# A graph layer pair on one Trainium2 core: neighbour mask by VectorE, distances between the message halves, convolution one group ahead

## The chip, the cores and the metric

The kernel runs on one core of one Trainium2 chip. The metric is the device time of one execution in microseconds (us). Everything is float32.

## The reference

For 128 graphs of 128 nodes with 256 features, two layers follow one another, each with a residual. Layer 0, cut to what is computed:

```python
h = maximum(layernorm(x), 0)
c = relu(bn1(conv1(h)))                       # 1x1
x_conv = relu(bn2(conv2(c)) + h)              # 17 taps along the nodes
s = h @ w_se.T + b_se                         # 3 values per node
A = exp(-(|s_n|^2 + |s_m|^2 - 2 s_n.s_m)) * adj
x_nmp = A @ relu(h @ w_msg.T + b_msg)
gi = concat(x_conv, x_nmp) @ w_ih.T + b_ih    # three gates
gh = h @ w_hh.T + b_hh
r, z = sigmoid(gi_r + gh_r), sigmoid(gi_z + gh_z)
n = tanh(gi_n + r * gh_n)
x = x + (1 - z) * n + z * h
```

Layer 1 normalizes again and runs two graph convolutions on five fixed subsets of the first 25 nodes of each graph (53 rows in all), with `adj` restricted to them, and adds the weighted results to those nodes.

## The kernel before, in words

The graphs are taken in 32 groups of four (`q`, `GB = 4`). The 17-tap convolution is done in a Fourier basis of 80 samples, so that it becomes matrix products per frequency.

The stages:

- **A** (`stage_a`, two batches of 16 groups): normalize, transpose to `hT`, first convolution, transform to `X`.
- **B** (`stage_b`, per batch): the products per frequency (L526) with weights streamed from DRAM (`wf`, issued on SP at L512), results `yd` to DRAM.
- **Neighbours** (`early` and `neighbours`, L608 to L675): runs beside A and B and at the start of C, one group at a time. It loads `hT` and the mask `ad` (L571 to L576, the mask as 128 partitions of 4 x 128), computes embeddings `pse` (L614), their products `ef` (ScalarE, L618) and `lr` (VectorE, L621), both halves of the messages (L630, L633, L635), then the distances `pd` (L643), four TensorE transposes of the mask into the other half of the same banks (L645), the exponentials (L647), the multiply by the mask read from PSUM (L648), and the sum over neighbours `px` (L656, L658), written to DRAM.
- **C** (`stage_c`, one group at a time, two generators open): the inverse transform `pi` (L706), 32x32 block transposes on VectorE (L711), scale, add and relu to `xc` (L716, L719), and then the gates as fast products of 2x2 blocks with seven products: `part` (L730) issues the matmuls of one of them (all at L735), `bank` (L744) takes one of three PSUM banks of pool `pgat` or one of five of `ptmp`. The first matmuls of the gates are the early part of `p1`, `p6` and `p5` with operands `hT` and `xm` (L761 to L764), then the part of `p1` that needs `xc` (L765). `u2` is a copy of `p1` by ScalarE (L766). After the three `wh` products (L781 to L786) the matmuls of L788 add to the same bank `p1`. At the end of a group come tanh (L855) and six GpSimd operations (L858 to L861, for each of two halves: subtract, multiply, add), whose tile `d` has the tag `u3` or `u2` (L857); the next group's `u2` uses that tile again. Transposes of the result (`po`, L878) and the output follow at least 11 planner microseconds later.
- **Layer 1** (`rows`, `prepare`, `block`, blocks of 16 graphs): runs beside C on what is finished. `gather` (L1075) multiplies 64x64 blocks of the normalized mask `ac` with 64-row slices of `zt`; `fuse` (L1086) adds them up per node.

What sets the order: the program is written out by hand through generators. `Order.run` (L183) takes, among the lanes, the one with the least work done for its weight whose next step is due; a step yields its planned TensorE time and the delay until the next step is due. With delay 0.0 a lane stays due. Layer 1's lane has weight 0.2; the `early` lane 0.2 to 0.66 in A and B and 0.5 in C. Each engine then runs its own instructions strictly in that order, and so does each DMA queue: SP carries nearly all loads, POOL the stores.

Buffers: pools give a tag a fixed number of tiles; a new tile waits until the last reader of the one before is done. `u2`, `u3`, `tc`, `r`, `z`, `xt` have one tile, `yt` two, `hTc` three.

Of the kernel before, what the change touches and what calls it, by code (L numbers as in the profile page):

```python
# [9 lines left out]
FP = mybir.dt.float32  # L10
AF = mybir.ActivationFunctionType
ALU = mybir.AluOpType
# [8 lines left out]
GB = 4  # L21
# [71 lines left out]
def _constants():  # L93
# [30 lines left out]
    for r, (n, g) in enumerate(zip(row_node, row_group)):  # L124
        for s in range(2):
            k = s * RP + r
            parts["et"][n, k] = 1
            parts["same"][k, [i for i in range(NR) if row_group[i] == g]] = 1
            parts["diag"][k, r] = 1
            for j in (s, s + 2):  # L130
                parts["e4"][k, j * WIDE + n] = 1
            parts["s2"][k, s * WIDE + n] = 1
            parts["grp"][k, g] = 1
            parts["sgrp"][k, s * NG + g] = 1
            parts["grpt"][g, k] = 1
# [72 lines left out]
def kernel(ctx: ExitStack, tc: tile.TileContext, x, adj, consts, vecs, w_se, conv1_w,  # L208
# [362 lines left out]
    def load_n(q):  # L571
        hT = LATE["io"].tile([P, 2, 512], FP, tag="hT", name=f"hT{q}")
        nc.sync.dma_start(out=hT, in_=hTd[q])
        ad = LATE["io"].tile([P, GB, N], FP, tag="adj", name=f"adj{q}")
        nc.sync.dma_start(out=ad, in_=adj[q * GB:(q + 1) * GB].rearrange("b n m -> n b m"))
        return hT, ad  # L576

    SUMS = {}
# [29 lines left out]
    def neighbours(q, hT, ad, xm):  # L608


        pse = ptmp.tile([P, 512], FP, tag="tmp", name=f"pse{q}")
        for k in range(2):
            for j in range(GB):
# [8 lines left out]
        yield 0.5, 0.0  # L622

        msgs = []
        for h in range(2):
            pm = ptmp.tile([P, 2, D], FP, tag="tmp", name=f"pm{q}_{h}")
            for i in range(2):
                j = 2 * h + i
                for k in range(2):
                    nc.tensor.matmul(pm[:, i], hT[:, k, j * N:(j + 1) * N], LATE["wmsg"][:, k],  # L630
                                     start=(k == 0), stop=(k == 1))
            msg = LATE["fr"].tile([P, 2, D], FP, tag=f"msg{h}", name=f"msg{q}_{h}")
            nc.vector.tensor_tensor(  # L633
                msg, pm, LATE["bmsg"][:, None, :].to_broadcast([P, 2, D]), ALU.add)
            nc.scalar.activation(msg, msg, AF.Relu)  # L635
            msgs.append(msg)
            yield 1.75, 0.0

        pds = [ptmp.tile([P, 2, N], FP, tag="tmp", name=f"pd{q}_{j}") for j in range(GB)]
        aT = LATE["fr"].tile([P, GB, N], FP, tag="aT", name=f"aT{q}")  # L640
        for j in range(GB):
            rows = slice(j * WIDE, (j + 1) * WIDE)
            nc.tensor.matmul(pds[j][:, 0], lr[rows, 0], lr[rows, 1], start=True, stop=True)  # L643
        for j in range(GB):
            nc.tensor.transpose(pds[j][:, 1], ad[:, j], ident)  # L645
        for j in range(GB):
            nc.scalar.activation(aT[:, j], pds[j][:, 0], AF.Exp)  # L647
            nc.vector.tensor_mul(aT[:, j], aT[:, j], pds[j][:, 1])  # L648
        yield 0.9, 3.0


        for h in range(2):
            px = ptmp.tile([P, 2, 2, N], FP, tag="tmp", name=f"px{q}_{h}")
# [30 lines left out]
        yield 0.0, 7.0  # L684
        IN[q] = hT, xm

    def stage_c(q):
        while not (q - 1 in G_DONE and q in IN):
            yield 0.0, 0.5
        some_sums(q, None)  # L690
        (hT, xm), (th, tm, _) = IN.pop(q), SUMS.pop(q)

        if (q, 0) not in IN2:
            load_yt(q, 0)
            load_yt(q, 1)
            yield 0.0, 6.0
        fr = LATE["co"]
        xi = fr.tile([P, 2, 512], FP, tag="tc", name=f"xi{q}")
        xc = fr.tile([P, 2, 512], FP, tag="xc", name=f"xc{q}")
        for h in range(2):  # L700
            yt = IN2.pop((q, h))
            pi = ptmp.tile([P, 2, 2, 4, WIDE], FP, tag="tmp", name=f"pi{q}_{h}")
            for n in range(4):
                o = n % 2 * WIDE
                for w in range(4):
# [2 lines left out]
                        inv[:F, o:o + WIDE],  # L708
                        yt[:, n // 2::2].rearrange("f g (k w c) -> w f g k c", k=2, w=4)[w],
                        start=True, stop=True)  # L710
            nc.vector.transpose(xi[:, :, h * D:(h + 1) * D],  # L711
                                pi.rearrange("p k g n c -> p k (g n c)"))
            load_yt(q + 1, h)
            s = slice(h * D, (h + 1) * D)
            for co in range(2):
                nc.vector.scalar_tensor_tensor(xc[:, co, s], xi[:, co, s],  # L716
                                               scl["bn2"][:, co:co + 1], hT[:, co, s],
                                               op0=ALU.mult, op1=ALU.add)
                nc.scalar.activation(xc[:, co, s], xc[:, co, s], AF.Relu,  # L719
                                     bias=sft["bn2"][:, co:co + 1])  # L720
        yield 1.8, 0.0

        wrz, wn, wh = LATE["wrz"], LATE["wn"], LATE["wh"]

# [34 lines left out]
        r1, r2 = r[:, :, :D], r[:, :, D:]  # L759
        early = [(0, hT, th), (2, xm, tm)]  # L760
        p1, p6, p5 = bank(wrz, 0), bank(wrz, 5), bank(wrz, 4)  # L761
        for ps, i in ((p1, 0), (p6, 5), (p5, 4)):
            part(ps, wrz, i, early, True, False)
            yield 1.75, 0.0  # L764
        part(p1, wrz, 0, xs[2:], False, True)  # L765
        nc.scalar.activation(u2, p1, AF.Copy)  # L766
        tcs, todo = sums("tc", q, xc)
        for operation in todo:
            operation()
        yield 0.87, 0.0  # L770
        xs, xh = [(0, hT, th), (2, xm, tm), (1, xc, tcs)], [(0, hT, th)]

        ve = fr.tile([P, 3, 1, D], FP, tag="ve", name=f"ve{q}")
# [22 lines left out]
        part(p5, wrz, 4, xs[2:], False, True)  # L796
        some_sums(q + 1, 2)
        yield 0.87, 0.0
        while q and q - 1 not in C_DONE:
            yield 0.0, 0.5  # L800
        z = fr.tile([P, 2, 512], FP, tag="z", name=f"z{q}")
# [145 lines left out]
    def prepare(blk):  # L947

        while not (blk - 1 in P_DONE and blk - 2 in {-2, *B1_DONE}):
# [1 line left out]
        pool, pool2, b1 = S["pool"], S["pool2"], S["b1"]  # L951
        ac, r4 = S["ac"][blk % 2], S["r4"][blk % 2]
        aj = pool.tile([NN, SB, NN], FP, tag="dd", name=f"aj{blk}")
        nc.sync.dma_start(out=aj, in_=adj[blk * SB:(blk + 1) * SB, :NN, :NN]
                          .rearrange("b n m -> n b m"))
        yield 0.0, 4.0

        for r, n, w in _runs():
# [43 lines left out]
                         start=True, stop=True)  # L1002
        for j in range(GB):
            s = slice(j * WIDE, (j + 1) * WIDE)
            nc.vector.tensor_copy(r4[s, :, j, :], pr4[s, :, j // 2, :NR])
        yield 0.9, 1.0
        P_DONE.add(blk)

    def block(blk):
# [64 lines left out]

        def gather(q):  # L1075
            zt = zts[q]
            pg2 = ptmp.tile([P, 2, D], FP, tag="tmp", name=f"pg2{blk}_{q}")
            for a in range(2):
                for s in range(2):
                    rows = slice(s * RP, (s + 1) * RP)  # L1080
                    nc.tensor.matmul(pg2[rows, a], ac[rows, 2 * q + a], zt[rows, a],  # L1081
                                     start=True, stop=True)
            nc.vector.tensor_tensor(zt, pg2, b2row[:, None, :].to_broadcast([P, 2, D]), ALU.add)
            nc.scalar.activation(zt, zt, AF.Relu)

        def fuse(q):  # L1086
            zt = zts.pop(q)
            pf = ptmp.tile([P, D], FP, tag="tmp", name=f"pfu{blk}_{q}")
            for a in range(2):
                nc.tensor.matmul(pf[a * 2 * WIDE:(a + 1) * 2 * WIDE], s2w, zt[:, a],  # L1090
                                 start=True, stop=True)
            nc.vector.tensor_add(x1[:, q], x1[:, q], pf)
            b0 = blk * SB + q * GB
# [7 lines left out]
        for what, q in ((turn, 0), (turn, 1), (turn, 2), (gather, 0), (turn, 3), (gather, 1),  # L1101
                        (gather, 2), (fuse, 0), (gather, 3), (fuse, 1), (fuse, 2), (fuse, 3)):
            what(q)
            if (what, q) == (gather, QS - 1):
                B1_DONE.add(blk)
            yield {turn: 0.45, gather: 0.9, fuse: 0.5}[what], 0.5
        F_DONE.add(blk)


# [70 lines left out]
```

## Time and profile before

| | |
|---|---|
| median of three runs | 2049.64 us (2045.02 to 2052.85) |
| the profiled execution | 2049.36 us, of which the span of the core is 2047.5 us |
| granted TensorE clock, mean | 0.995 |
| DMA packets | 190148, 281.91 MB |
| mean share of the DMA engines, first 18 of 40 slices | 0.4 to 0.9 or more |
| mean share of the DMA engines, last 22 of 40 slices | 0.1 to 0.3 |

How to read the views: a group of instructions is given by its source line, engine and operation, with the number of instructions, their busy time and mean duration. A float32 matmul is recorded as two MATMUL records (two passes), a transpose as one. Durations of neighbouring matmuls overlap, so the time that a stretch of matmuls takes is read from start to start: 256 columns take 0.216 us a pass. A wait is "who, at which line, waited for whom". L735 holds all gate matmuls, which are told apart by their operands (`hTc`, `xm`, `xc`, `th`, `tm`, `tc`) and weights (`wrz`, `wn`, `wh`).

Where each stage lies: the neighbour stage from 164 us to about 803 us; stage C from 679.5 us (first `pi`) on, with one group every 34 to 51 us in its steady part; layer 1 from about 840 us; the last block of layer 1 alone from 2000 us.

### The profile page before, as it was taken

What the parts mean: (1) busy time and instruction counts of PE and PEld (TensorE: products, weight loads), DVE (VectorE), ACT (ScalarE), POOL (GpSimd) and SP (SyncE); (2) the same over time, 40 slices, a digit from 0 to 9 for tenths busy, and PEclk for the clock granted to TensorE, in tenths of its full rate; (3) what the DMA queues carried; (4) which work ended last, traced back from release to release, by engine and by line L of the source; (5) the groups of instructions that cost most, each with busy time, mean ns of one, the idle gap of its engine ahead of it and who ended that gap; (6) DMA issues with size and microseconds to landing.
All of it is one profiled execution on the core that took longest, in us unless ns stands there. A gap on an engine that the chain in (4) does not pass through costs nothing.

```text
span 2047.5 us, 34132 instructions
## 1 busy us (share of the span) xinstructions
PE 2006.3 (98%) x12852; PEld 1659.2 (81%) x12852; DVE 1285.1 (63%) x2775; ACT 688.5 (34%) x1547; POOL 741.3 (36%) x898
## 2 busy tenths in 40 slices
PE   7998999999999999999999999999999999999998
PEld 5667888888888888878788788878888888878875
DVE  6774445875433676757756776777567667766742
ACT  4663222454222344222222332232232323222333
POOL 3552665333655032422422233233224323233230
PEclk9999999999999999999999999999999999999999
DMA  9997788645777544431323232332332233323121
GB/s 217 295 284 229 265 267 281 191 162 185 253 256 245 152 127 131 116 108 53 87 73 91 75 84 83 101 80 76 83 88 78 76 98 90 86 78 104 39 71 52
DMA packets 190148, 281.91 MB, mean 138 GB/s; under 512 B 23626, under 2 KB 143375, under 8 KB 189983
## 3 DMA queue, kind: packets, MB, share of 16 engines
q1 hardware_dynamic: 156942, 185.46, 31.7%
q0 software_dynamic: 32656, 93.98, 14.5%
q8 instruction: 102, 1.67, 0.3%
q14 instruction: 64, 0.52, 0.1%
q10 hardware_dynamic: 384, 0.28, 0.1%
HBM read 187.34 MB, written 92.27 MB: 137 GB/s over the span
## 4 chain that ended last, share of the span: by engine, by line
PE 89%; DVE 3%; issue 3%; POOL 3%; DMA 2%; ACT 1%; SPq 0%; POOLq 0%; DVEq 0%; ACTq 0%
PE p L735 39%; PE pa L526 7%; PE pm L630 5%; PE ph L1038 5%; PE pz L1047 5%; PE pc L421 4%; PE pb L526 3%; PE pf L432 3%; PE px L656 3%; PE pi L706 3%; PE pg L1081 1%; PE pw L474 1%; PE po L878 1%; PE ph L410 1%; PE py L1021 1%
## 5 line engine op out<-in xcount | busy, mean ns | idle before, releaser
L858 POOL TENSOR_TENSOR d<-hTc,r 128x512 f32<-128x512 f32 x64 | 87.2, 1362 | 299.3 <-ACT r L855 288.7
L526 PE MATMUL pa<-wf,X 128*128 128x256 f32 x640 | 152.2, 381 | 0.0
L716 DVE SCALAR_TENSOR_TENSOR xc<-xi,s_bn,hTc 128x256 f32<-128x256 f32 x128 | 148.1, 1195 | 2.3
L558 DVE SCALAR_TENSOR_TENSOR y<-pa,kk 128x512 f32<-128x512 f32 x78 | 53.8, 690 | 151.4 <-ACT kk L557 151.4
L887 POOL DMA_DIRECT2D out<-xt x128 | 72.2, 569 | 172.5 <-DVE xt L884 169.3
L750 ACT ACTIVATE z<-z,brz 128x256 f32<-128x256 f32 x128 | 58.1, 501 | 221.3 <-DVE z L804 187.9
L735 PE MATMUL p<-tm,wrz 128*128 128x256 f32 x512 | 132.3, 381 | 0.0
L735 PE MATMUL p<-th,wrz 128*128 128x256 f32 x512 | 132.1, 380 | 0.0
L735 PE MATMUL p<-tc,wrz 128*128 128x256 f32 x512 | 131.8, 380 | 0.0
L526 PEld LDWEIGHTS pa<-wf,X 128*128 128x128 f32 x640 | 118.1, 190 | 16.2 <-issue 2.0
L630 PE MATMUL pm<-wmsg,hT 128*128 128x256 f32 x512 | 123.3, 386 | 0.0
L421 PE MATMUL pc<-c1w,hTa 128*128 128x256 f32 x512 | 121.4, 383 | 1.2 <-ACT hTa L412 1.2
L1040 ACT ACTIVATE hh<-ph,vec 128x96 f32<-128x96 f32 (+3 forms) x160 | 64.4, 403 | 147.0 <-PE ph L1038 137.8
L1038 PE MATMUL ph<-yz,w 128*128 128x96 f32 (+3 forms) x640 | 110.5, 327 | 1.9 <-issue 1.0
L719 ACT ACTIVATE xc<-xc,t_bn 128x256 f32<-128x256 f32 x128 | 64.8, 508 | 138.8 <-DVE xc L716 138.8
L630 PEld LDWEIGHTS pm<-wmsg,hT 128*128 128x128 f32 x512 | 97.3, 193 | 15.8 <-ACT kk L557 1.4
L421 PEld LDWEIGHTS pc<-c1w,hTa 128*128 128x128 f32 x512 | 94.3, 191 | 18.2 <-DVE h L424 4.8
L735 PEld LDWEIGHTS p<-tm,wrz 128*128 128x128 f32 x512 | 97.8, 191 | 13.5
L735 PE MATMUL p<-hTc,wrz 128*128 128x256 f32 x384 | 103.9, 393 | 5.0 <-ACT u L766 4.9
L735 PEld LDWEIGHTS p<-th,wrz 128*128 128x128 f32 x512 | 97.1, 190 | 13.6 <-PE p L735 0.2
L1038 PEld LDWEIGHTS ph<-yz,w 128*128 128x128 f32 x640 | 89.0, 195 | 23.3 <-issue 16.5
L1047 PE MATMUL pz<-hh,w 128*128 128x96 f32 (+3 forms) x640 | 107.3, 321 | 0.0
(200 smaller groups left out, 4566.1 us busy)
## 6 DMA issues: line engine op xcount, KB each, us to landing
wf<-wfd SPq DMA_DIRECT2D x160, 256.0 KB, 3.2
wfd<-ws POOLq DMA_DIRECT2D x64, 320.0 KB, 8.9
yd<-y POOLq DMA_DIRECT2D x80, 256.0 KB, 4.1
yt<-yd SPq DMA_DIRECT2D x64, 320.0 KB, 4.9
w<-in_W SPq DMA_DIRECT2D x40, 512.0 KB, 4.0
xa<-in_x SPq DMA_DIRECT2D x128, 128.0 KB, 5.2
hTd<-hTa POOLq DMA_DIRECT2D x32, 512.0 KB, 5.9
hT<-hTd SPq DMA_DIRECT2D x32, 512.0 KB, 6.3
```

Of the source, the lines that this page charges most:

```text
L421: nc.tensor.matmul(pc[:, i], hT[:, k, (2 * h + i) * N:(2 * h + i + 1) * N], c1w[:, k], start=(k == 0), stop=(k == 1))
L432: nc.tensor.matmul(pf[:, i, :F * NB], h1[:, 2 * h + i, k * P:(k + 1) * P], fwd, start=True, stop=True)
L526: nc.tensor.matmul(ps, xk(k), WF[f][:, k, s], start=(k == 0), stop=(k == 1))
L630: nc.tensor.matmul(pm[:, i], hT[:, k, j * N:(j + 1) * N], LATE["wmsg"][:, k], start=(k == 0), stop=(k == 1))
L716: nc.vector.scalar_tensor_tensor(xc[:, co, s], xi[:, co, s], scl["bn2"][:, co:co + 1], hT[:, co, s], op0=ALU.mult, op1=ALU.add)
L719: nc.scalar.activation(xc[:, co, s], xc[:, co, s], AF.Relu, bias=sft["bn2"][:, co:co + 1])
L735: nc.tensor.matmul(ps[:, m], w[:, i, k, m * P:(m + 1) * P], factor(i, x, t), start=first and j == 0, stop=last and j == len(n) - 1, skip_g ...
L858: nc.gpsimd.tensor_sub(d, hT[:, dc], r[:, dc])
L887: nc.gpsimd.dma_start(out=out[q * GB + j, WIDE:].rearrange("(t n) c -> n t c", n=WIDE), in_=xt[j * WIDE:(j + 1) * WIDE, 1:4])
L1038: nc.tensor.matmul(ph, w1[:, k, m * P:(m + 1) * P], yz[:, k, :, o:o + n], start=(k == 0), stop=(k == 1))
L1040: nc.scalar.activation(hh[:, m], ph, AF.Relu, bias=v("b1", g * 4 + m))
L1047: nc.tensor.matmul(pz, w2[:, g, m, cc * P:(cc + 1) * P], hs[g][:, m], start=(m == 0), stop=(m == 3))
```

## The change

1. *Mask*: it is loaded by four DMAs of 32 partitions, with runs of 32 elements, so that partition w*32+n holds the 32-column block w of rows n, n+32, n+64, n+96 of each graph. One VectorE instruction at the head of `neighbours` transposes all 32x32 blocks into a new tile `adT`. The four TensorE transposes are gone, and the mask is multiplied from SBUF, two graphs at a time.
2. *Order in neighbours*: distances and exponentials stand between the first and the second half of the messages.
3. *Stage C*: the inverse transform up to `xc` becomes a generator-free function `convolved`, called for group q+1 in the middle of group q (after the `xc` part of `p5`) if that group's inputs are there, otherwise at its own head; `xc` has two tiles and is transposed in place. At the head of a group `p1` is computed whole, copied, and only then come the early parts of `p6` and `p5`.
4. *Layer 1*: the pairs of graphs in the packed order are exchanged (`e4`, the `aj` load in four DMAs, `r4`), so that `gather`'s four matmuls use four different quadrants of the array and two PSUM banks, with two VectorE adds of 256 columns instead of one of 512.

```diff
@@ -127,7 +127,7 @@
             parts["et"][n, k] = 1
             parts["same"][k, [i for i in range(NR) if row_group[i] == g]] = 1
             parts["diag"][k, r] = 1
-            for j in (s, s + 2):
+            for j in (2 * s, 2 * s + 1):
                 parts["e4"][k, j * WIDE + n] = 1
             parts["s2"][k, s * WIDE + n] = 1
             parts["grp"][k, g] = 1
@@ -571,8 +571,11 @@
     def load_n(q):
         hT = LATE["io"].tile([P, 2, 512], FP, tag="hT", name=f"hT{q}")
         nc.sync.dma_start(out=hT, in_=hTd[q])
-        ad = LATE["io"].tile([P, GB, N], FP, tag="adj", name=f"adj{q}")
-        nc.sync.dma_start(out=ad, in_=adj[q * GB:(q + 1) * GB].rearrange("b n m -> n b m"))
+        ad = LATE["io"].tile([P, GB * 4, WIDE], FP, tag="adj", name=f"adj{q}")
+        for w in range(4):
+            nc.sync.dma_start(out=ad[w * WIDE:(w + 1) * WIDE],
+                              in_=adj[q * GB:(q + 1) * GB, :, w * WIDE:(w + 1) * WIDE]
+                              .rearrange("b (k n) m -> n (b k) m", n=WIDE))
         return hT, ad
 
     SUMS = {}
@@ -608,6 +611,9 @@
     def neighbours(q, hT, ad, xm):
 
 
+        adT = LATE["fr"].tile([P, GB, N], FP, tag="adT", name=f"adT{q}")
+        nc.vector.transpose(adT.rearrange("p b n -> p (b n)"),
+                            ad.rearrange("p b n -> p (b n)"))
         pse = ptmp.tile([P, 512], FP, tag="tmp", name=f"pse{q}")
         for k in range(2):
             for j in range(GB):
@@ -622,7 +628,8 @@
         yield 0.5, 0.0
 
         msgs = []
-        for h in range(2):
+
+        def message(h):
             pm = ptmp.tile([P, 2, D], FP, tag="tmp", name=f"pm{q}_{h}")
             for i in range(2):
                 j = 2 * h + i
@@ -634,20 +641,21 @@
                 msg, pm, LATE["bmsg"][:, None, :].to_broadcast([P, 2, D]), ALU.add)
             nc.scalar.activation(msg, msg, AF.Relu)
             msgs.append(msg)
-            yield 1.75, 0.0
-
-        pds = [ptmp.tile([P, 2, N], FP, tag="tmp", name=f"pd{q}_{j}") for j in range(GB)]
+
+        message(0)
+        yield 1.75, 0.5
+        pds = [ptmp.tile([P, N], FP, tag="tmp", name=f"pd{q}_{j}") for j in range(GB)]
         aT = LATE["fr"].tile([P, GB, N], FP, tag="aT", name=f"aT{q}")
         for j in range(GB):
             rows = slice(j * WIDE, (j + 1) * WIDE)
-            nc.tensor.matmul(pds[j][:, 0], lr[rows, 0], lr[rows, 1], start=True, stop=True)
+            nc.tensor.matmul(pds[j], lr[rows, 0], lr[rows, 1], start=True, stop=True)
         for j in range(GB):
-            nc.tensor.transpose(pds[j][:, 1], ad[:, j], ident)
-        for j in range(GB):
-            nc.scalar.activation(aT[:, j], pds[j][:, 0], AF.Exp)
-            nc.vector.tensor_mul(aT[:, j], aT[:, j], pds[j][:, 1])
-        yield 0.9, 3.0
-
+            nc.scalar.activation(aT[:, j], pds[j], AF.Exp)
+            if j % 2:
+                nc.vector.tensor_mul(aT[:, j - 1:j + 1], aT[:, j - 1:j + 1], adT[:, j - 1:j + 1])
+        yield 0.45, 0.0
+        message(1)
+        yield 1.75, 0.3
 
         for h in range(2):
             px = ptmp.tile([P, 2, 2, N], FP, tag="tmp", name=f"px{q}_{h}")
@@ -684,19 +692,11 @@
         yield 0.0, 7.0
         IN[q] = hT, xm
 
-    def stage_c(q):
-        while not (q - 1 in G_DONE and q in IN):
-            yield 0.0, 0.5
-        some_sums(q, None)
-        (hT, xm), (th, tm, _) = IN.pop(q), SUMS.pop(q)
-
-        if (q, 0) not in IN2:
-            load_yt(q, 0)
-            load_yt(q, 1)
-            yield 0.0, 6.0
-        fr = LATE["co"]
-        xi = fr.tile([P, 2, 512], FP, tag="tc", name=f"xi{q}")
-        xc = fr.tile([P, 2, 512], FP, tag="xc", name=f"xc{q}")
+    XC = {}
+
+    def convolved(q, hT):
+
+        xc = XC[q] = LATE["co"].tile([P, 2, 512], FP, tag="xc", name=f"xc{q}", bufs=2)
         for h in range(2):
             yt = IN2.pop((q, h))
             pi = ptmp.tile([P, 2, 2, 4, WIDE], FP, tag="tmp", name=f"pi{q}_{h}")
@@ -708,17 +708,31 @@
                         inv[:F, o:o + WIDE],
                         yt[:, n // 2::2].rearrange("f g (k w c) -> w f g k c", k=2, w=4)[w],
                         start=True, stop=True)
-            nc.vector.transpose(xi[:, :, h * D:(h + 1) * D],
-                                pi.rearrange("p k g n c -> p k (g n c)"))
             load_yt(q + 1, h)
             s = slice(h * D, (h + 1) * D)
+            nc.vector.transpose(xc[:, :, s], pi.rearrange("p k g n c -> p k (g n c)"))
             for co in range(2):
-                nc.vector.scalar_tensor_tensor(xc[:, co, s], xi[:, co, s],
+                nc.vector.scalar_tensor_tensor(xc[:, co, s], xc[:, co, s],
                                                scl["bn2"][:, co:co + 1], hT[:, co, s],
                                                op0=ALU.mult, op1=ALU.add)
                 nc.scalar.activation(xc[:, co, s], xc[:, co, s], AF.Relu,
                                      bias=sft["bn2"][:, co:co + 1])
-        yield 1.8, 0.0
+
+    def stage_c(q):
+        while not (q - 1 in G_DONE and q in IN):
+            yield 0.0, 0.5
+        some_sums(q, None)
+        (hT, xm), (th, tm, _) = IN.pop(q), SUMS.pop(q)
+
+        if q == 0:
+            load_yt(q, 0)
+            load_yt(q, 1)
+            yield 0.0, 6.0
+        fr = LATE["co"]
+        if q not in XC:
+            convolved(q, hT)
+            yield 1.8, 0.0
+        xc = XC.pop(q)
 
         wrz, wn, wh = LATE["wrz"], LATE["wn"], LATE["wh"]
 
@@ -759,15 +773,15 @@
         r1, r2 = r[:, :, :D], r[:, :, D:]
         early = [(0, hT, th), (2, xm, tm)]
         p1, p6, p5 = bank(wrz, 0), bank(wrz, 5), bank(wrz, 4)
-        for ps, i in ((p1, 0), (p6, 5), (p5, 4)):
-            part(ps, wrz, i, early, True, False)
-            yield 1.75, 0.0
-        part(p1, wrz, 0, xs[2:], False, True)
+        part(p1, wrz, 0, xs, True, True)
         nc.scalar.activation(u2, p1, AF.Copy)
         tcs, todo = sums("tc", q, xc)
         for operation in todo:
             operation()
-        yield 0.87, 0.0
+        yield 2.6, 0.0
+        for ps, i in ((p6, 5), (p5, 4)):
+            part(ps, wrz, i, early, True, False)
+            yield 1.75, 0.0
         xs, xh = [(0, hT, th), (2, xm, tm), (1, xc, tcs)], [(0, hT, th)]
 
         ve = fr.tile([P, 3, 1, D], FP, tag="ve", name=f"ve{q}")
@@ -796,6 +810,9 @@
         part(p5, wrz, 4, xs[2:], False, True)
         some_sums(q + 1, 2)
         yield 0.87, 0.0
+        if q + 1 in IN:
+            convolved(q + 1, IN[q + 1][0])
+            yield 1.8, 0.0
         while q and q - 1 not in C_DONE:
             yield 0.0, 0.5
         z = fr.tile([P, 2, 512], FP, tag="z", name=f"z{q}")
@@ -951,8 +968,10 @@
         pool, pool2, b1 = S["pool"], S["pool2"], S["b1"]
         ac, r4 = S["ac"][blk % 2], S["r4"][blk % 2]
         aj = pool.tile([NN, SB, NN], FP, tag="dd", name=f"aj{blk}")
-        nc.sync.dma_start(out=aj, in_=adj[blk * SB:(blk + 1) * SB, :NN, :NN]
-                          .rearrange("b n m -> n b m"))
+        for i in range(GB):
+            nc.sync.dma_start(out=aj[:, i % 2 * 2 + i // 2::GB],
+                              in_=adj[blk * SB + i:(blk + 1) * SB:GB, :NN, :NN]
+                              .rearrange("b n m -> n b m"))
         yield 0.0, 4.0
 
         for r, n, w in _runs():
@@ -1002,7 +1021,7 @@
                          start=True, stop=True)
         for j in range(GB):
             s = slice(j * WIDE, (j + 1) * WIDE)
-            nc.vector.tensor_copy(r4[s, :, j, :], pr4[s, :, j // 2, :NR])
+            nc.vector.tensor_copy(r4[s, :, j % 2 * 2 + j // 2, :], pr4[s, :, j % 2, :NR])
         yield 0.9, 1.0
         P_DONE.add(blk)
 
@@ -1074,20 +1093,21 @@
 
         def gather(q):
             zt = zts[q]
-            pg2 = ptmp.tile([P, 2, D], FP, tag="tmp", name=f"pg2{blk}_{q}")
+            pg2 = [ptmp.tile([P, D], FP, tag="tmp", name=f"pg2{blk}_{q}_{s}") for s in range(2)]
             for a in range(2):
                 for s in range(2):
                     rows = slice(s * RP, (s + 1) * RP)
-                    nc.tensor.matmul(pg2[rows, a], ac[rows, 2 * q + a], zt[rows, a],
-                                     start=True, stop=True)
-            nc.vector.tensor_tensor(zt, pg2, b2row[:, None, :].to_broadcast([P, 2, D]), ALU.add)
+                    nc.tensor.matmul(pg2[s][a * RP:(a + 1) * RP], ac[rows, 2 * q + a],
+                                     zt[rows, a], start=True, stop=True)
+            for s in range(2):
+                nc.vector.tensor_add(zt[:, s], pg2[s], b2row)
             nc.scalar.activation(zt, zt, AF.Relu)
 
         def fuse(q):
             zt = zts.pop(q)
             pf = ptmp.tile([P, D], FP, tag="tmp", name=f"pfu{blk}_{q}")
-            for a in range(2):
-                nc.tensor.matmul(pf[a * 2 * WIDE:(a + 1) * 2 * WIDE], s2w, zt[:, a],
+            for s in range(2):
+                nc.tensor.matmul(pf[s * 2 * WIDE:(s + 1) * 2 * WIDE], s2w, zt[:, s],
                                  start=True, stop=True)
             nc.vector.tensor_add(x1[:, q], x1[:, q], pf)
             b0 = blk * SB + q * GB
@@ -1103,7 +1123,7 @@
             what(q)
             if (what, q) == (gather, QS - 1):
                 B1_DONE.add(blk)
-            yield {turn: 0.45, gather: 0.9, fuse: 0.5}[what], 0.5
+            yield {turn: 0.45, gather: 0.5, fuse: 0.5}[what], 0.5
         F_DONE.add(blk)
```

## Prediction before the run

> **What bounds the kernel now.** I read the page's busy shares and the chain of work that ended last first, then the waits, then the timeline of one group boundary.
>
> ```profile
> PE 2006.3 (98%) x12852; PEld 1659.2 (81%) x12852; DVE 1285.1 (63%) x2775; ACT 688.5 (34%) x1547; POOL 741.3 (36%) x898
> ...
> PE 89%; DVE 3%; issue 3%; POOL 3%; DMA 2%; ACT 1%; SPq 0%; POOLq 0%; DVEq 0%; ACTq 0%
> ```
>
> TensorE is the bound: a microsecond of matmuls removed, or of waiting added to its queue, moves the end. VectorE (63%), ScalarE and GpSimd matter only where TensorE waits for them. The waits name such a place:
>
> ```profile
> PE p L735 <- ACT u L766: 4.9, 7, 1.8
> ...
> PEld p L735 <- ACT u L766: 11.6, 17, 2.2
> ...
> ACT u L766 <- POOL z L861: 17.5, 17, 2.0
> ```
>
> Columns: microseconds in all, times, longest. In stage_c `u2` (L766) is a copy of bank `p1`; the matmuls of L788 add to that bank again ("p1 again") and wait for the copy. `u2`'s tile is the one the previous group's `d` used (L857, tag u2), so the copy waits for the last of six GpSimd operations (L858 to L861, two rounds) of the group before. The timeline at a boundary, TensorE first:
>
> ```profile
> 1569.98 0.59 PE L735 MATMUL p<-xc,wn 128*128 128x256 f32 x2
> 1570.51 1.95 PE L706 MATMUL pi<-yt,cst 80*32 80x128 f32 x64
> 1572.39 1.13 PE L735 MATMUL p<-hTc,wrz 128*128 128x256 f32 x4
> ...
> 1577.67 1.03 PE L735 MATMUL p<-xc,wrz 128*128 128x256 f32 x4
> ...
> 1578.97 1.03 PE L735 MATMUL p<-th,wh 128*128 128x256 f32 x4
> 1579.95 1.13 PE L735 MATMUL p<-hTc,wrz 128*128 128x256 f32 x4
> ```
>
> Starts are what counts (durations overlap): the old group ends at 1570.51, and p1 again starts 9.44 us later. GpSimd and ScalarE meanwhile:
>
> ```profile
> 1571.00 1.29 POOL L858 TENSOR_TENSOR d<-hTc,r 128x512 f32<-128x512 f32 x1
> ...
> 1577.95 1.32 POOL L861 TENSOR_TENSOR z<-d,r 128x512 f32<-128x512 f32 x1
> ```
>
> ```profile
> 1579.30 0.60 ACT L766 ACTIVATE u<-p 128x512 f32<-128x512 f32 x1 [0.61 <-POOL z L861]
> ```
>
> GpSimd ends 8.76 after the boundary, the copy 0.6 later, p1 again 0.05 after that. So the nine microseconds of matmuls ahead of p1 again just cover the GpSimd chain: the cover is used up.
>
> **What the Trainium skill says.** *TensorEngine Tiling (Array Packing)*, Key Properties: "Tiles operate independently", and a 64x64 mode has four. The trace agrees on the principle: L474, on four row slices with a bank each, takes 1.03 us from start to start for 8 passes of 512 columns, where two full-array passes of that width (L996) take 0.86. Four 64x64 tiles at once are not in this trace. *SBUF — State Buffer*, Two separate sides: VectorE with two SBUF inputs and a GpSimd operation that reads SBUF exclude each other. The trace agrees: L716 takes 477 ns at least, 1483 in the median, beside the GpSimd chain. *VectorE: DVE Perf Modes*, The three transpose paths: VectorE transposes 32x32 blocks only, which is why the change has to load the mask as blocks. *DMA: Bandwidth & Descriptors*, Why small descriptors are slow: a fixed cost per packet. Here a 512-byte packet takes 27 ns in the median and a 100-byte one 13.
>
> **The change, part by part.** Sums are made against the profiled execution, 2049.4 us (span 2047.5); the median of the runs, 2049.6, is 0.3 above.
>
> *Mask transposes leave TensorE.* Four of L645 for each of 32 groups. Start to start (L645 at 661.03, the next work at 661.52) a set takes 0.49: 32 x 0.49 = **-15.7**, all on the bound.
>
> *Mask transposed by VectorE.* One 128x512 transpose, priced by L711 (706 ns), and two 128x256 multiplies (some 420 ns by L834) instead of four of 279 (L648): +0.4 us a group, 14 us on an engine that is idle 37%. Nothing on the path. If GpSimd holds the port, a multiply of two SBUF tiles can take 1.5 as L716 does; the second half of the messages (1.73) and mostly 2.6 us of stage B stand ahead of its reader.
>
> *Mask loads.* 512 packets of 512 bytes become 2048 of 128: priced between 13 and 27 ns, nearer 13, about 32 x (2048 x 14 - 512 x 27)/16 = 29 us of the 16 engines spread over 600 us. SP issues four DMAs where it issued one (0.43 each): +1.3 a group ahead of the `wf` loads, on a queue that mostly waits for free buffers. But the VectorE transpose stands at the head of the group, and a late mask would hold back `lr`, the message adds and other lanes' work queued on VectorE. From group 1 on the mask is issued 13 us or more ahead of the embedding matmuls; for group 0 only 3.6. Value: 1 us for group 0.
>
> *Distances between message halves.* `lr` is ready 2.2 us after the embedding matmuls (4.1 in stage B beside GpSimd). Ahead of the distances stand now 1.9 of messages, and, where another lane is due, 2.6 more. Bounds: -4 (the few waits on `aT` and in L643 vanish) to +10 (0.3 in each group). Value 0, because both sides have few places without a filler.
>
> *Gather on four quadrants.* Four 64x64 matmuls of two passes run in pairs now: 1559.42 to 1560.44, 1.02 us. With four at once two passes of 0.216 and a mode switch are left, an estimate of 0.58 by L1090 (two 64-column tiles, the same four records). 0.43 x 32 = -13.8 at best, 0 if they don't overlap. In the last block the extra VectorE add (2 x 0.42 for 0.69) eats it: I take 28 x 0.43 = **-12.0**. The relabelled `e4`, `r4` and 24 more small `aj` loads: nothing, prepare has microseconds ahead of it.
>
> *Convolution of the next group moved up.* The 64 records of L706 (1.88), two transposes, four L716 and four L719 move from the head of group q+1 to the middle of group q, with their two `yt` loads, which pass the `xt` loads on SP. Neither loads late: `yt` has a whole group's time. Away from the GpSimd chain L716 should fall from 1195 to about 480 ns; since VectorE was hidden, that is worth nothing by itself. In its new place VectorE needs some 3.2 us, beside 1.88 + 2.59 of matmuls ahead of L803: covered.
>
> *The order at the head of a group.* This is the part that decides. Ahead of p1 again there will be p1 whole (12 passes, 2.59), p6 and p5 early (3.46) and the `wh` products (1.30): 7.35 us after the boundary instead of 9.33. GpSimd's chain doesn't move with it: it starts from the old group's tanh, and its six operations need 6 x 1.27 + 0.3 = 7.9 even alone (last group), 8.35 beside VectorE now. I take 0.1 off, since the four L716 go and the four `tc` subtractions stay. I read the boundary of every group q from 1 to 31. In 27 no other lane's matmul stands between boundary and p1 again, because those steps end in yields with no delay and a lane is passed over only when its next step isn't due; the new yields are of that kind too. In these 27 GpSimd ends 6.8 to 9.5 us after the boundary. Its end plus 0.6 for copy and hand-over, less 7.27, gives a wait of 0.1 to 0.3 in seven and of 1.3 to 2.8 (mean 2.2) in twenty: **+45.1**. Today's wait at this place, start to start, is 7.6 in 17 boundaries and is contained in that: **-7.6**.
>
> Sum: 2049.4 - 15.7 - 12.0 + 1 + 45.1 - 7.6 = **2060**. What is late next after the copy: `va` (L783) behind it on ScalarE, then L785 and L786, which h1's second use needs only 3.5 us later.
>
> **Rivals.** *The wait stays covered* (faster). If other lanes' steps land ahead of p1 again, or tanh comes early enough as at the seven light boundaries, only the savings count: 2049.4 - 27.7 = 2022; with half the wait covered, 2049.4 - 27.7 + 1 + 22.5 - 7.6 = 2038. For it: at seven of 27 boundaries GpSimd is early. Against it: the cause is layer-two work ahead of the last matmuls, whose pattern I see no reason to change.
> *Gather not four at once*: 2060 + 12 = 2072. For it: no such tile set in the trace. Against: row slices and column slices each overlap.
> *VectorE in the way* (slower, forecast's wait besides): if the moved convolution finds VectorE behind and L803, L804 come late, p5 isn't free for its next product. From some 1 us of lateness on it costs; at 0.7 a group, 31 x 0.7 = 22: 2082. Against: that much cover is there.
>
> **How the numbers follow.** Forecast 2060, chance 0.52, own range 2047 to 2073 (wait 45 +/- 9, gather 0 to -13.8). Covered wait 0.15 near 2022, half covered 0.12 near 2038; gather in pairs 0.12; VectorE late 0.09. Half a per cent, 10.2 us, is what a measurement of this kernel can tell from no change: below 2039.4 the covered wait and a part of the half-covered, 0.19; between, the rest of it and some of the lower half of the forecast's own range, 0.31; above 2059.9, 0.50. The range 2034 to 2078 leaves 0.12 below and 0.07 above.
>
> **What would show it.** TensorE's busy matmul work down by the L645 set and gather sets of about 0.58; waits of p1's second use on the `u` copy, and of that on GpSimd, up from 17 us to 40 or more, with p1 again still some 9.4 us after the boundary; the moved L716 near 480 ns. The prediction is wrong if that wait doesn't grow, if other lanes' matmuls stand ahead of p1 again, or if a wait appears on the mask loads or behind the moved convolution.

## The result, and the profile after

The changed kernel takes 2142.12 us in the median of four runs (2139.97 to 2148.12), beside 2049.0 of the kernel before in the same comparison: 1.0459 times, 95% interval 1.043 to 1.0489. The prediction was 2060 with a range to 2078: the side was right, the size was not. The profiled execution of after took 2142.74 us, with a span of 2140.9.

Page of after, busy time of the engines and chain that ended last:

```profile
PE 2018.8 (94%) x12724; PEld 1659.2 (78%) x12724; DVE 1301.4 (61%) x2775; ACT 665.4 (31%) x1537; POOL 739.6 (35%) x898
...
PE 70%; POOL 12%; issue 8%; DVE 3%; ACT 3%; DMA 2%; SPq 1%; POOLq 0%; ACTq 0%; DVEq 0%
```

TensorE is busy 12.5 us longer than before with 128 records fewer (the mask transposes), and GpSimd has taken 12% of the chain where it had 3%. So matmuls became slower as well as waiting. The mean granted clock says the same. It was 0.995 before; after has:

```profile
core 0: 2140.9 us, clock 0.976
```

A lost clock of 0.024 x 2140.9 is 51 us of full speed, idle time included, against 10 us before. In the record of the granted clock, before has five stretches at half clock, 23.8 us together, and after has 22, 104.0 together. Part of that falls on idle time of TensorE, where it costs nothing (16.4 us of it in the gap at 735 us, shown below): at half clock TensorE was busy for 15.1 us before and for 75.6 us after. Half of that is lost, 7.5 and 37.8 us, and the difference is worth **30 us**. The prediction has no such term.

Waits of TensorE in after (in all, times, longest):

```profile
PE p L749 <- ACT u L777: 43.0, 26, 2.8
PE pi L706 <- DMA yt<-yd: 21.6, 1, 21.6
PE prow L301 <- DVE wide L300: 9.7, 1, 9.7
PE pse L620 <- DMA hT<-hTd: 6.5, 1, 6.5
PE pd L651 <- DVE lr L627: 5.4, 4, 3.3
PE ph L410 <- DVE h L424: 4.0, 1, 4.0
```

The first is the predicted one. Lines 3 and 4 were there before, with 10.0 and 6.3. The second is new, and before shows the last two nowhere at this size. At the boundary of group 16, TensorE:

```profile
1397.61 0.66 PE L1100 MATMUL pg<-zt,ac 64*64 64x256 f32 x8
1398.20 0.70 PE L749 MATMUL p<-tm,wn 128*128 128x256 f32 x2
...
1400.47 1.03 PE L749 MATMUL p<-hTc,wrz 128*128 128x256 f32 x4
...
1406.95 1.03 PE L749 MATMUL p<-th,wh 128*128 128x256 f32 x4
1410.15 1.34 PE L749 MATMUL p<-hTc,wrz 128*128 128x256 f32 x4 [2.18 <-ACT u L777]
1411.29 1.91 PE L749 MATMUL p<-xm,wrz 128*128 128x256 f32 x4
1412.99 1.70 PE L749 MATMUL p<-xc,wrz 128*128 128x256 f32 x4
```

GpSimd and ScalarE:

```profile
1401.09 1.47 POOL L875 TENSOR_TENSOR d<-hTc,r 128x512 f32<-128x512 f32 x1 [12.95 <-ACT r L872]
...
1408.21 1.26 POOL L878 TENSOR_TENSOR z<-d,r 128x512 f32<-128x512 f32 x1
```

```profile
1409.50 0.60 ACT L777 ACTIVATE u<-p 128x512 f32<-128x512 f32 x1 [7.65 <-POOL z L878]
```

The group begins at 1400.47, GpSimd ends at 9.0 after that, the copy ends 0.6 later, p1 again starts at 9.7: the chain of the prediction. The `L1100` line is the gather: the set takes 0.59 from start to start. New is what follows the wait. Four passes of 256 columns take 0.86 from start to start; from 1410.9 on they take 1.70. The table of stretches (length, busy us of PE, PEld, DVE, ACT, POOL, then granted clock, DMA share, GB/s) shows why:

```profile
1406.00:1410.90 4.90, 2.72 (x13) 2.07 (x12) 0.42 (x1) 0.87 (x2) 3.31 (x3) 1.00 0.00 0
1410.90:1414.30 3.40, 3.40 (x10) 2.65 (x9) 0.42 (x1) 0.00 (x0) 0.00 (x0) 0.51 0.00 0
```

For 3.4 us after the wait the clock is halved, which costs another 1.7 us. Of the twenty waits of 1.5 us and more at this place eight are followed, 0.5 to 0.8 us after their end, by such a stretch. The other twelve, of 1.5 to 3.0, are not.

What tells them apart stands in the record of the granted clock. All 22 stretches of after begin on marks that lie 3.413 us apart: those at 1066.2, 1281.2, 1318.8 and 1410.9 are 63, 11 and 27 such intervals from each other. In the eight cases at least 2.16 us of idle time lie between two marks; in the other twelve a mark divides the wait, or it is short, and no interval has more than 1.89. Here are the interval with the wait above, and the two that share the wait of 1447.0 to 1449.0, after which the clock stays full:

```profile
1407.53:1410.94 3.41, 1.23 (x7) 0.76 (x6) 0.43 (x2) 0.87 (x2) 1.86 (x2) 1.00 0.00 0
1445.07:1448.48 3.41, 1.92 (x9) 1.33 (x8) 0.80 (x1) 0.11 (x1) 3.11 (x3) 1.00 0.00 0
1448.48:1451.90 3.42, 2.88 (x13) 2.57 (x14) 0.84 (x2) 0.76 (x2) 0.00 (x0) 1.00 0.00 0
```

Six more of the 22 stretches follow no idle time at all. Before each of them one interval holds the whole of this work of layer 1, which uses 25 of the array's rows (`25*128`; with `L994` after it, it takes 2.16 us from start to start):

```profile
1315.61 1.99 PE L989 MATMUL pa<-cst,b 25*128 25x64 f32 x16
```

It comes eight times in each kernel. In before it lies whole in an interval three times, and just these three are followed by a stretch; the two that a mark divides in after are not. Over all fifteen traces, from 150 us on, 113 of the 115 full-speed intervals with 2.15 us or more of idle time or of this work are followed by half clock, and 16 of some 8070 others. So a kernel's share of half clock depends in part on where its work falls between the marks.

The second place is the start of stage C:

```profile
728.95 1.03 PE L526 MATMUL pb<-wf,xs 128*128 128x256 f32 x4
751.55 3.64 PE L706 MATMUL pi<-yt,cst 80*32 80x128 f32 x64 [21.57 <-DMA yt<-yd]
```

Stage B ends at 729.6 and the first `pi` starts 21.9 us later. Before, those were 663.9 and 679.5, and the 15.6 us between were filled by neighbour groups: 7 of 32 had not yet begun, and the last began at 790. In after the last began at 686.8 and nothing is left. SP's queue:

```profile
732.01 0.33 SPq L920 DMA_DIRECT2D b2s<-in_b  x1
732.42 0.96 SPq L943 DMA_DIRECT2D w<-in_W  x2
733.48 0.60 SPq L246 DMA_DIRECT2D w<-in_W  x1
734.13 7.13 SPq L689 DMA_DIRECT2D hTc<-hTd  x1
741.31 0.43 SPq L691 DMA_DIRECT2D xm<-xmd  x1
741.78 13.76 SPq L608 DMA_DIRECT2D yt<-yd  x4
```

The weights of layer 1, whose loads start when the neighbours are done, are now issued ahead of `yt` and share the DMA engines with it (busy to 0.98 between 729.8 and 751.5). `yt` is issued 12.2 us after stage B's end (before: 1.5). A half-clock stretch of 23.9 us begins in this gap, at 735.1.

### The profile page after: what moved, and what is told of

The parts are those of the page before. It is cut to its first block, busy times and chain, and to the rows that moved or that the text cites. A ratio compares the mean times of both kernels' runs of the same rounds, so it can differ in the third digit from the quotient of the medians.

```text
span 2140.9 us, 34046 instructions
## 1 busy us (share of the span) xinstructions
PE 2018.8 (94%) x12724; PEld 1659.2 (78%) x12724; DVE 1301.4 (61%) x2775; ACT 665.4 (31%) x1537; POOL 739.6 (35%) x898
## 2 busy tenths in 40 slices
DMA packets 240956, 281.92 MB, mean 132 GB/s; under 512 B 90817, under 2 KB 194182, under 8 KB 240790
## 4 chain that ended last, share of the span: by engine, by line
PE 70%; POOL 12%; issue 8%; DVE 3%; ACT 3%; DMA 2%; SPq 1%; POOLq 0%; ACTq 0%; DVEq 0%
PE p L749 25%; PE pa L526 6%; PE pm L637 6%; PE ph L1057 5%; PE pz L1066 4%; PE pc L421 4%; POOL d L876 4%; POOL z L878 4%; POOL d L875 3%; PE pb L526 3%; PE pf L432 3%; PE px L664 3%; PE pi L706 2%; PE pw L474 1%; PE ph L410 1%
## 5 line engine op out<-in xcount | busy, mean ns | idle before, releaser
L904 POOL DMA_DIRECT2D out<-xt x128 | 72.1, 569 | 236.3 <-DVE xt L901 233.3
L637 PE MATMUL pm<-wmsg,hT 128*128 128x256 f32 x512 | 132.5, 404 | 2.8 <-DVE msg L640 0.3
L749 PEld LDWEIGHTS p<-hTc,wrz 128*128 128x128 f32 x384 | 71.4, 194 | 68.7 <-ACT u L777 56.2
L1057 PE MATMUL ph<-yz,w 128*128 128x96 f32 (+3 forms) x640 | 115.2, 338 | 1.0 <-issue 1.0
L718 ACT ACTIVATE xc<-xc,t_bn 128x256 f32<-128x256 f32 x128 | 58.1, 500 | 186.2 <-DVE xc L715 186.2
L1057 PEld LDWEIGHTS ph<-yz,w 128*128 128x128 f32 x640 | 94.0, 205 | 21.6 <-issue 15.0
L749 PE MATMUL p<-xm,wrz 128*128 128x256 f32 x384 | 107.3, 405 | 0.0
```

The costliest lines, as they stand in the source:

```text
L749: nc.tensor.matmul(ps[:, m], w[:, i, k, m * P:(m + 1) * P], factor(i, x, t), start=first and j == 0, stop=last and j == len(n) - 1, skip_g ...
L904: nc.gpsimd.dma_start(out=out[q * GB + j, WIDE:].rearrange("(t n) c -> n t c", n=WIDE), in_=xt[j * WIDE:(j + 1) * WIDE, 1:4])
L1057: nc.tensor.matmul(ph, w1[:, k, m * P:(m + 1) * P], yz[:, k, :, o:o + n], start=(k == 0), stop=(k == 1))
```

## The experiments

Ratios are to the kernel before on the same chip, with 95% intervals; differences between runs are taken from the ratios where it says so. "Wait" is the sum at p1's second use less a pass and mode switch, over all groups (after: 48.5). "Half clock" is the sum of such stretches (after: 104.0; before: 23.8); "busy" behind it is the part in which TensorE works (75.6; 15.1), of which half is lost.

**The scratch of its own.** GpSimd's `d` goes into `xc`, which is dead by then, so the copy no longer waits for the group before:

```diff
-            d = fr.tile([P, 512], FP, tag=f"u{2 + dc}", name=f"d{q}_{dc}")
+            d = xc[:, 1 - dc]
```

> The changed kernel, but the GpSimd chain's scratch d lies in the finished xc tile instead of the u2/u3 tiles, so the copy of p1 no longer waits for GpSimd. Theory 1 (the wait at p1's second use, 48.5 us in the changed kernel, and the half-clock windows of 3.4 us that follow it, some 14 in stage C, 1.7 us each, cost most of the loss): the wait and those windows vanish, 2142 falls by 65 to 75 us to about 2070. Theory 2 (the wait is only what was forecast and the windows have another cause, such as the longer wait at the start of stage C): it falls by the wait alone, to about 2094. Theory 3 (the loss lies in the neighbour stage): within 10 us of 2142.

Measured: 2076.35 us, 1.0125 (1.0109 to 1.014). Wait 0.1, half clock 72.1, busy 39.0. TensorE at the same group:

```profile
1412.31 1.03 PE L749 MATMUL p<-hTc,wrz 128*128 128x256 f32 x4
...
1418.78 1.03 PE L749 MATMUL p<-th,wh 128*128 128x256 f32 x4
1419.64 0.59 PE L749 MATMUL p<-hTc,wrz 128*128 128x256 f32 x2
```

and its GpSimd:

```profile
1412.90 1.29 POOL L875 TENSOR_TENSOR xc<-hTc,r 128x512 f32<-128x512 f32 x1
...
1419.91 1.26 POOL L878 TENSOR_TENSOR z<-xc,r 128x512 f32<-128x512 f32 x1
```

p1 again starts 7.3 us after the group's begin, while GpSimd still works: the 7.35 of the prediction. The spans differ by 68.2 (2140.9 to 2072.7): 48.4 of wait and (75.6 - 39.0)/2 = 18.3 of clock make 66.7 of it. None of the eight stretches behind the wait is left; they are 13.7 of the 18.3. Four `L989` stretches fewer (6.8) are not owed to the wait: here a mark divides that work more often. Stretches elsewhere are some 2 us longer. So the wait is real and dearer than its length, and 1.25% over before come from elsewhere.

**Useless matmuls instead of the wait**, from group 1 on, after the `wh` products:

```diff
+        if q:
+            pad = bank(wh, 9, ptmp)
+            for _ in range(5):
+                nc.tensor.matmul(pad[:, 0], wh[:, 0, 0], hT[:, 0, :D], start=True, stop=True)
         part(p1, wrz, 1, xs, False, True, True)
```

> The changed kernel with five useless matmuls of 128x256 (2.16 us) put right before p1's second use in every group but the first, into a bank that nobody reads; the output is unchanged. TensorE is kept busy during the wait, which itself stays. If the waits cause the half-clock windows: about 14 windows go, 24 us less, and in the 9 or so groups that hardly waited 1.8 us more each, 16 us more: about 2134, and the mean clock up from 0.976 to 0.985. If the windows have another cause: 2158, clock unchanged.

Measured: 2151.16, 1.0491 (1.0476 to 1.0507), wait 3.2, half clock 78.7, busy 48.4. TensorE at a boundary:

```profile
1420.89 2.32 PE L805 MATMUL p<-hTc,wh 128*128 128x256 f32 x10
1423.23 1.13 PE L749 MATMUL p<-hTc,wrz 128*128 128x256 f32 x4
1424.20 1.03 PE L749 MATMUL p<-xm,wrz 128*128 128x256 f32 x4
```

No wait, and full speed behind it (0.86 for the four passes from 1424.20). The padding, 31 x 10 passes x 0.216 = 67, replaces 45 of waiting: +22, where +16 was expected. The clock gives (75.6 - 48.4)/2 = 13.6 back, where 24 was expected. The sum, 2142.1 + 22 - 13.6 = 2150.5, is close to the measured 2151.2, and the larger part of the miss is the clock: fourteen stretches were to go, and eight went. They are the eight behind the wait; the six at `L989` are still there. The idle time brings about these eight, and filling it with work takes them away.

**Stage C of before, the rest of after** (the diff's part 3 undone):

> The changed kernel with the stage C of before (convolution at the head of its own group, p1, p6, p5 early). Gather, mask and order in the neighbour stage stay as changed. Theory 1: wait back to about 8 us and few half-clock windows in stage C, 2142 - 41 - 24 = 2077; what is left above 2049 is the neighbour stage and the start of stage C. Theory 3 (the loss lies in the neighbour stage): about 2130.

Measured: 2073.04, 1.0117 (1.0099 to 1.0134), wait 2.8. TensorE's wait for `yt` at the start of stage C stays, with 20.5.

**Mask load and neighbours of before, the rest of after** (parts 1 and 2 undone):

> The changed kernel with the mask load and neighbour stage of before (TensorE transposes, distances after both message halves). If the new neighbour stage costs some 20 us of small waits in stages A and B and, by being finished before stage B, leaves nothing to cover the 21.7 us wait for yt at the start of stage C: 2142 + 15.7 - 20 - 21.7 - 7 for the clock there = about 2109. If these are only the same loss shown in another place: 2142 to 2158.

Measured: 2102.72, 1.0248 (1.0223 to 1.0273), wait 45.7; the wait for `yt` is gone. The two costs stand apart: stage C with its wait is worth 3.4% of before, the neighbour stage 2.1%.

**The neighbours of before, with gather, convolution ahead and the scratch in `xc`** (both edits above):

> The changed kernel with GpSimd's scratch in xc and the whole neighbour stage of before, TensorE transposes included: gather and the moved convolution without its wait. Both repairs at once: if they are independent, 2142 - 66 - 39 = 2037; by work, gather_only (2041) less 8 us of waits on the copy, 2033.

Measured: 2031.54, 0.9901 (0.988 to 0.9922). So, of the changed kernel, gather and convolution without their wait are a gain. Against the first experiment (1.0125) only the neighbour stage differs: 46 us by the ratios, 38.0 between the spans. The first `pi` waits 21.9 less and busy time at half clock falls from 39.0 to 23.3 (7.8 us lost less); 15.7 of transposes come back. That leaves 38.0 + 15.7 - 21.9 - 7.8 = 24 for waits inside the stage and in stage A beside it.

**The gather alone, on before:**

> The kernel before with only the gather part of the change (exchanged pairs, four quadrants, two banks, aj in four DMAs). By the forecast's step: 28 sets at 0.43 us less, 2049 - 12 = 2037. If the quadrant gather had a cost elsewhere (two adds for one, one bank more): within 5 us of 2049.

Measured: 2041.48, 0.9958 (0.9943 to 0.9973): 8.6 us. The gather's planned time goes from 0.9 to 0.5 with it, as in the change, so what that moves is in the 8.6; it was not tried apart. To the one above it lacks 11.7 (interval some 5 either way), of which the old wait (8.8 here) can be most.

**Gather and mask by VectorE on before, order of the neighbours kept.** The distances' step has its planned time cut as in the change:

```diff
-        yield 0.9, 3.0
+        yield 0.45, 3.0
```

> Gather and the mask by VectorE on the kernel before; the order of the neighbour stage is the one of before, distances after both halves of the messages, delay 3.0 after them. If the short-run loads and the transpose on VectorE are harmless and the loss of the neighbour stage lies in the new order: 2049 - 12 - 15.7 = 2021. If VectorE, held up by the mask loads or by GpSimd, is what costs: 2040 or more.

Measured: 2052.04, 1.0013 (1.0003 to 1.0024): 31 us more than expected. Half clock 55.6, busy 40.1; 30 groups had begun at stage B's end, where before 25 had.

**The same with the planned 0.9 kept:**

```diff
-        yield 0.45, 3.0
+        yield 0.9, 3.0
```

> Gather and the mask by VectorE on the kernel before, as in gather_mask, but the step that lost its transposes keeps its planned 0.9 us instead of 0.45, so that the planner puts all steps in the order of before. Theory P (the mask transposes do save 15.7 us, but the shorter plan lets the neighbour lane run ahead, so that its groups are used up before the bare stretches around the end of stage B): 2041 - 15.7 = 2026. Theory V (VectorE with the mask in its queue, or the short-run loads, cost as much as the transposes saved): unchanged, 2052.

Measured: 2031.61, 0.9906 (0.988 to 0.9931). One number of the plan, which issues no instruction, is worth some 22 us by the ratios, 19 between the spans. 25 groups had begun, half clock is 28.0, busy 18.0. The stretch 680 to 800 without and with it, in this order:

```profile
680.00:800.00 120.00, 110.59 (x750) 93.14 (x748) 74.90 (x145) 36.54 (x84) 36.54 (x45) 0.96 0.50 149
```

```profile
680.00:800.00 120.00, 119.09 (x801) 101.80 (x799) 81.05 (x160) 51.81 (x106) 23.25 (x25) 1.00 0.38 99
```

The mask on VectorE itself is a gain of some 11 us over the gather alone.

**The first experiment, layer 1 held back until `yt` is issued** (the first line stands behind group 0's two `load_yt`, the second in layer 1's setup):

```diff
+            STARTED.add(q)
-        while len(E_DONE) < NQ:
+        while len(E_DONE) < NQ or not STARTED:
```

> The kernel own_d (changed kernel, GpSimd's scratch in xc), with the setup of layer 1 (memsets and 3.6 MB of weight loads on SP) held back until stage C has issued its first yt loads. If the 22 us wait for yt at the start of stage C comes from standing behind those loads on SP: the wait falls to about 10 and the half-clock stretch after it goes, 2076 - 12 - 4 = 2060. If it is the latency of the loads themselves, which the neighbour groups used to cover: no change, 2076.

Measured: 2060.56, 1.0056 (1.0041 to 1.0071):

```profile
PE pi L706 <- DMA yt<-yd: 11.6, 1, 11.6
```

The wait for `yt` falls from 21.9 to 11.6, and half clock from 72.1 to 56.0 (busy from 39.0 to 33.3). So queueing behind layer 1's weights is about half of this wait; the other half is that no neighbour group covers it.

**The first experiment with the old neighbour order**, mask by VectorE, planned 0.45 and then 0.9:

> The kernel own_d with the neighbour stage's order of before (distances after both halves, delay 3.0) and the mask still by VectorE. If the order is the cause of the loss in stages A and B and of the bare start of stage C: 2049 - 12 - 15.7 - 7.6 = 2014. If the VectorE mask is: 2040 or more.

Measured: 2047.92, 0.9985 (0.9972 to 0.9999), where 2014 was expected: like the other 0.45.

> The kernel own_d_mask with the planned 0.9 us kept in the same way: gather, mask by VectorE, convolution one group ahead, GpSimd's scratch in xc, neighbour order of before. Theory P: the savings add up, 2026 less the 8.8 us of waits on the copy of p1 and their clock, about 2016. Theory V: 2048.

Measured: 2025.67, **0.9868 (0.9845 to 0.9892)**, faster than both kernels, though by the ratio some 6 us above what was expected. Its page:

```profile
PE 1978.7 (98%) x12724; PEld 1641.5 (81%) x12724; DVE 1317.3 (65%) x2775; ACT 682.6 (34%) x1547; POOL 742.8 (37%) x898
```

It has as many TensorE records as after, in 40 us less of busy time. Of these (75.6 - 17.8)/2 = 28.9 are the clock; the rest was not traced to its places.

**The new neighbour order with 0.9 for the distances** (on the first experiment):

> The kernel own_d (neighbour order of the change, distances between the message halves) with the planned 0.9 us kept for the step with the distances. If only the shorter plan harmed: about 2025. If the new order with its short delays (0.5 and 0.3 instead of 3.0) harms by itself, by running the neighbour lane ahead and by waits on lr and on banks: 2060 to 2076.

Measured: 2069.32, 1.0084 (1.0062 to 1.0106). The planned time is worth some 8 us here and is not enough: all 32 groups had begun before stage B's end, and the wait on `yt` stands at 21.7. Left is the delay ahead of the sum over neighbours, which the change cut from 3.0 to 0.3. Two causes are open, the order itself or its delay. With the delay put back:

```diff
         message(1)
-        yield 1.75, 0.3
+        yield 1.75, 3.0
```

> The kernel order_plan (new neighbour order, planned 0.9 kept, scratch in xc) with the delay after the second half of the messages set from 0.3 to the 3.0 that stood after the distances before. If the short delay is what lets the neighbour lane finish before stage B: fewer than 32 groups start before the end of stage B, the 21.8 us wait for yt goes, and 2069 falls to about 2045; the small waits of the new order, some 16 us, stay. If the order itself leads the lane ahead: 2069.

Measured: 2032.99, 0.9928 (0.9902 to 0.9954). By the ratio that is some 11 us better than the expected 2045; where these lie was not traced. 30 groups had begun, half clock is 32.1, no wait on `yt` is left among TensorE's waits. The delay was worth some 32 us by the ratios. The order itself still costs: with the same planned times and 0.5 less delay the old order has 0.9868, some 12 us less (the intervals do not overlap). Why more of its groups had begun at stage B's end, 30 for 25, stays open.

## Why the prediction was wrong, point by point

- *TensorE bounds, and p1 again waits for `u2`*: **right**. Forecast: a mean of 2.2 in twenty groups, 45.1 in all; measured: twenty of 1.5 to 3.0 with a mean of 2.2, 48.5 in all. The working subtracts 7.27 where its own sum gives 7.35 (7.33 in the first experiment), some 2 us of the 45.1.
- *Transposes away from TensorE, -15.7; mask by VectorE and its loads free*: **nearly right**. The set is gone; 11 (5 to 17) came in with the plan kept. The transpose takes 702 ns and the multiply 420 in the median. VectorE waits 7.6 us for the mask of group 0, once, and TensorE's wait at that place stays as before.
- *Gather, -12 at a set of 0.58*: **right** in the set, 0.59; the gain, 8.6 us (5.5 to 11.7), is a little less.
- *Convolution moved up, covered*: **right**. L715 is at 482 ns in the median, where L716 had 1483. *SBUF — State Buffer* of the Trainium skill, Two separate sides, on which the prediction rested here, agrees with that. TensorE's waits on VectorE in stage C are 7.0 in all (1.7 before), far from the 22 of the rival.
- *Distances between message halves, value 0, -4 to +10*: **the step that failed first**. I looked at the data each step waits for, and at nothing of what the plan does with the steps. With the three new yields a group has 6.25 us of planned work in place of 6.7, and 0.8 of delay in place of 3.0. So the lane ran ahead of stage B and was used up when stage B ended. The start of stage C, where it had been the cover, lay bare: 21.7 us, and a long half-clock stretch there, of which 7.4 us fell on busy time. The order adds small waits: from start to start in after, 7.7 us where `pm` follows `pd` (31 times 0.25), 4.4 where `pd` follows `pm`, 3.2 between `pd`s; before has some 5 in the same places. That these 0.25 are a bank of `ptmp` not yet free was argued from code and waits, not tried.
- *The price of a wait*: **the second failure**. I took a wait at its length, and the clock at nothing; it was 30 us, 13.7 of it behind these waits. *TensorE: Matmul & The Clock Gate* of the Trainium skill, Part 1, What's actually happening, has the mechanism: the default is a throttled clock at half rate, released by sustained activity in a window of some 3.4 us. The trace agrees on rate and length (0.51 for 3.4 us). Its section HAM oscillation — how this bites in real kernels gives the rule of no idle gap above some 3.4 us; here gaps of 2.2 were enough in eight of twenty cases, so the measurement decides. The eight are those that lie between two marks.

The sum between the spans, by these readings: 2047.5 - 15.7 - 8.6 + 40.9 (wait, less the old 7.6) + 30.3 (clock) + 21.7 (`yt`) + 15.3 (small waits) = 2131.4, measured 2140.9. The 9.5 between are open. Two waits in stage A are left out of the sum, both of `ph`: the 4.0 on VectorE shown above, and one of 3.5. Against them stand the 5 us that before has at the places of the small waits, and the -15.7 and -8.6 were measured within 6 and 3 only. The prediction had 2060; 30 of clock and 37 of the neighbour stage are most of the miss.

## What to carry to other kernels

Before a stretch of matmuls is moved or dropped, ask which chain on another engine it covers, and when that chain starts. In an order made by a plan, the planned time and the delay of a step belong to the change: cutting one to the true cost moves every later step, and what ran out too early is missing where it was the filler. A wait of 2.2 us on a busy TensorE is to be counted with up to 1.7 us more for the clock, as is a stretch of such narrow matmuls, and a reading of the mean granted clock of before and after shows at once whether that happened.

## What was not expected of the hardware

- Half-clock stretches after waits of only 2.2 us, where these lie between two marks 3.413 us apart, and fewer when useless matmuls fill them (104.0 to 78.7 us in all; 59.6 to 31.0 after 790 us, where stage C is steady).
- Four 64x64 tiles at once, with two passes of 256 columns each, take 0.59 us from start to start where two pairs took 1.02.
- Mask loads in runs of 32 elements, 240956 packets in all for 190148, left no trace in TensorE's waits.
- Sixteen matmuls of 64 columns on 25 rows, though TensorE shows no idle time in them, brought half clock as a wait of that length does, in six of eight cases in after and in three of eight in before.
